# Two attention blocks over eight images: layer 1's first convolution in halves twice, its factors on GpSimd during attention, small norm products on GpSimd

## The chip, the cores and the metric

The kernel runs on one core of a Trainium2 chip. A core has five engines that work side by side, each with a queue that it takes in order: TensorE (PE: matmuls, with the weight loads shown as PEld), VectorE (DVE), ScalarE (ACT), GpSimd (POOL) and SyncE (SP), which here issues nearly all DMAs. They wait for each other by semaphores. The metric is the device time of one execution in microseconds. Before the change it is 2917.71 us, the median of three runs (2915.55 to 2919.3).

## The reference

The input is x with 8 images of 512 channels and 32 x 32 = 1024 positions, all in float32. Two layers follow each other:

```
layer 0:  h = group_norm(x, 32 groups);  q, k, v = w_qkv h + b   (8 heads of 64 channels)
          a = softmax(q^T k / 8) v for each head
          x = x + w_proj a + b_proj
layer 1:  h = group_norm(x, 8 groups)
          a = softmax(q^T k / sqrt(512)) v   (one head of 512 channels; q, k, v from 1x1 convolutions of h)
          out = x + w_p a + b
```

A 1x1 convolution is a product of a 512 x 512 weight with a 512 x 1024 image. In layer 1 the kernel multiplies weights once at the start: `m` joins those of q and k, so that the scores are h^T (m^T h), and `z` joins those of v and p. Layer 1 thus needs a first convolution g = m h (with the bias `ubias`), the scores of g and h, and a product with z.

## The kernel before, in words

**Products in seven instead of eight.** A product whose factors are cut in halves both ways takes eight products of the halves. `wino` (L227) makes it of seven, by Strassen's scheme in Winograd's form, from sums of halves: `left_sums` (L151) and `right_sums` (L165) give the steps: four kinds, each for two channel tiles, so eight additions or subtractions of 128x512 for an image. `image_factors` (L340) does that for an image with VectorE's `tensor_sub`. `conv` (L394) is a convolution that is halved once: seven products of four matmuls of 512 columns. A float32 matmul shows as two records in the profile, so that one product is eight records.

**Halved twice.** `conv2` (L416) halves each of the seven products again: 49 products of 128 x 128 weights with 256 columns. It takes them in four pairs: products 1 and 5, then 2 and 6, then 7 alone, then 3 and 4. Each pair goes through seven inner products; their results are added into the output tiles by VectorE (L439, from PSUM and from SBUF), with copies by ScalarE, and in the pair of product 7 by GpSimd as well (`more`, L443). It needs `inner_factors` (L400): for each of the seven outer factors four subtractions of 128x256, all on GpSimd (L411), and weights that `keep2` (L296) prepares once and stores in DRAM, read back in two parts. Before the change only layer 0's k and q convolutions are done so (of images 1 to 7); v, p, m and z are halved once. The bias is put on afterwards by ScalarE (`biased_half`, L446), one half of two output tiles at a time.

**Order of the work.** The loop over images b (L923) runs one stage after another: layer 0's attention of image b (`attention0`, L573), layer 1's first convolution of image b-1 (`layer1_scores`, L887), layer 0's projection of image b, the scores, z and the last product of image b-1, and v, k and q of image b+1. In the last round the previous image's layer 1 comes as always, and then that of the last image alone.

TensorE's matmuls are pinned to the order of the code (`matmul`, L66). The other engines' instructions are ordered by a planner of the language, which takes the earliest in the code that is ready by its own estimate, unless `tc.keep_in_program_order` pins one behind what stands before it on its engine. `background` is a list of small steps, of which a few are emitted after each product; `hooks` are steps emitted at given products; the last two products of a `wino` or of a pair wait in `tail` until the next one has begun.

**Attention of layer 0.** There are eight blocks (four pairs of heads, two halves of the queries). A block emits 16 score matmuls in eight steps, each followed by one exponential of 128x1024 on ScalarE (L590), whose results VectorE adds to a running total (L592, L594); then 16 matmuls with v; then `reciprocals` (L544): a matmul `sums` of the total with ones, VectorE's reciprocal `rc`, its minimum and (on GpSimd, L557) its sum kept for a check at the end, a DMA of `rc` to DRAM and back spread over partitions as `r`, and GpSimd's multiplication of the output by `r` (L611). The last block's multiplication is left to VectorE (`scaled`, L613). `extra` is a list of sixteen slots, two for each block: one emitted after the scores, one after the products with v. Before the change the slots 3, 5, 7 and 9 hold ScalarE's normalization (L140) of the next image to be treated, `h`; in image 0's attention the slots 0 to 6 hold the sums of the weights p, m and z, their stores (`keep`) and the first weight loads (`later`, L793).

**Memory.** All image tiles come from one pool of 32 buffers of 128x1024 (`big`, NBIG = 32, L19); weights from a pool of three (`wpool`). `uses` (L310) lists in which order the weights are loaded; each `load_weight` loads the next. PSUM pools are opened anew for each stage by `psum_pools` (L198).

**The norm.** `GroupNorm.affine` (L123) adds EPS on VectorE, takes the power -1/2 on GpSimd (L128), and then makes scale `s` and shift `b` by three VectorE instructions of 128x4 (L130, L132, L134).

Of the kernel before, what the change touches and what calls it, by code (L numbers as in the profile page):

```python
# [12 lines left out]
ALU = mybir.AluOpType  # L13
# [16 lines left out]
def two_attention_blocks_kernel(  # L30
# [41 lines left out]
    def pcols(name):  # L72
        i = 4 * PARAMS.index(name)
        return par[:, i : i + 4]
# [14 lines left out]
    class GroupNorm:  # L89
# [33 lines left out]
        def affine(self, ps):  # L123
            matmul(ps, gm[:, self.layer, :], self.dv, start=True, stop=True)
            ve = small.tile([P, KC], F32, tag="ve", name=f"ve_{self.uid}")
            nc.vector.tensor_scalar(ve, ps, EPS, None, ALU.add)  # L126
            rstd = small.tile([P, KC], F32, tag="rstd", name=f"rstd_{self.uid}")
            nc.gpsimd.tensor_tensor(rstd, ve, mhalf, ALU.pow)  # L128
            self.s = small.tile([P, KC], F32, tag="s", bufs=4, name=f"s_{self.uid}")
            nc.vector.tensor_mul(self.s, rstd, pcols(f"gn_w{self.layer}"))  # L130
            ms = small.tile([P, KC], F32, tag="ms", name=f"ms_{self.uid}")
            nc.vector.tensor_mul(ms, self.gmean, self.s)  # L132
            self.b = small.tile([P, KC], F32, tag="b", bufs=4, name=f"b_{self.uid}")
            nc.vector.tensor_sub(self.b, pcols(f"gn_b{self.layer}"), ms)  # L134

# [40 lines left out]
    def main_path(ctx):  # L176
# [113 lines left out]
        def keep(n, t):  # L290
            nc.sync.dma_start(wdram[n], t)


        wdram2 = {n: dram.tile([P, 7, 7, P], F32, name=f"sums2_{n}") for n in "qk"}

# [13 lines left out]

        twice = [("k", 0), ("k", 1), ("q", 0), ("q", 1)]  # L310
        uses = ["v", "p", *twice] if B > 1 else ["p"]
        for b in range(1, B):
            uses += ["m", "p", "z"] + (["v", *twice] if b + 1 < B else [])
        uses += ["m", "z"]
        loaded = []

        def load_weight():
            if uses:
                n = uses.pop(0)
                t = wpool.tile([P, 7 * C], F32, tag="w", name=f"w_{n[0]}_{len(uses)}")  # L320
                if n in twice:
                    t = t.rearrange("p (i j m) -> p i j m", i=4, j=7)
                    i = n[1]
                    t = t[:, : 4 - i]
                    nc.sync.dma_start(t, wdram2[n[0]][:, 4 * i : 4 + 3 * i])
                else:
                    t = t.rearrange("p (i k m) -> p i k m", i=7, k=2)
                    nc.sync.dma_start(t, wdram[n])
                loaded.append((n, t))
# [9 lines left out]

        def image_factors(h, uid):  # L340

            tiles = [pair_tile(f"t{i}_{uid}") for i in (1, 2, 4)]
            halves = lambda t: (t[:, :HT], t[:, HT:])
            return right_sums(
                [halves(t) for t in h[:2]], [halves(t) for t in h[2:]],
                [lambda j, t=t: t[:, j, :] for t in tiles], nc.vector.tensor_sub,
            )
# [67 lines left out]

        def conv2(n, f, bias, name, hooks=()):  # L416

# [28 lines left out]
            def biased_half(i, c):  # L446
                if bias is not None:
                    for r in range(2):
                        oc = 2 * i + r
                        t = out[oc][:, ts(c, HT)]  # L450
                        nc.scalar.activation(t, t, AF.Identity, bias=bias[:, oc : oc + 1])

# [86 lines left out]
            pair(2, (7,), [(1, 0)], [(0, 1)], [lambda: biased_half(1, 1)])  # L539
            pair(3, (3, 4), [(0, 1), (1, 0)], [(0, 1), (1, 0)], [load_weight, lambda: biased_half(0, 1), lambda: biased_half(1, 0)])  # L540
            return out
# [206 lines left out]
        def prologue():  # L748
# [44 lines left out]
            later = []  # L793
            for n in "pmz":
                t, steps = prepare(n)
                later.append(steps)
                later.append([lambda n=n, t=t: keep(n, t), load_weight])
            later.append([
                lambda: tc.keep_in_program_order(nc.vector.tensor_copy(ubias, bias[0])),
                lambda: tc.keep_in_program_order(nc.vector.tensor_add(obias[1], bias[1], pcols("bp1"))),  # L800
                lambda: tc.keep_in_program_order(nc.vector.tensor_add(obias[0], bias[2], pcols("bp0"))),
            ])
            return v, q, k, norm1, later

# [72 lines left out]
        def keys_and_queries(b, f, norm, hooks):  # L877

            k = conv2("k", f, None, f"k0_{b}", hooks)
            hooks = [[all_background], [], []]  # L880
            if norm:
                hooks[1].append(lambda: norm.group_mean(acc_tile(f"gmean_0_{b + 1}")[:, :KC]))
                hooks[2].append(lambda: norm.affine(acc_tile(f"gvar_0_{b + 1}")[:, :KC]))
            q = conv2("q", f, pcols("bq0"), f"q0_{b}", hooks)
            return q, k

        def layer1_scores(b, h, hooks):  # L887
            hf, steps = image_factors(h, f"h1_{b}")
            background.extend(steps)
            g = conv(  # L890
                weight("m"), hf, ubias, f"g1_{b}", middle=(2, 5, 6, 7), hooks=hooks, back=4,
                after=[load_weight, lambda: background.extend(gsteps)],
            )
            stiles = [pair_tile(f"sg{i}_{b}") for i in (1, 2, 4)]
            halves = lambda t: (t[:, :HT], t[:, HT:])
            gf, gsteps = left_sums(
                [halves(t) for t in g[:2]], [halves(t) for t in g[2:]],
                [lambda j, t=t: t[:, j, :] for t in stiles], nc.vector.tensor_add, nc.vector.tensor_sub,
            )
            return hf, gf  # L900

# [21 lines left out]
        for b in range(B):  # L923
# [11 lines left out]
            for i, f in enumerate(applies):  # L935
                extra[2 * i + 3].append(f)
            psum_pools(f"attention_{b}", 1)
# [4 lines left out]
            if b > 0:  # L942
                hf, gf = layer1_scores(b - 1, h, ends)
                norm1 = projection(b, af, xt)
# [6 lines left out]
                if b + 1 < B:  # L951
                    v, f, norm0 = values(b + 1, h)
                    q, k = keys_and_queries(b + 1, f, norm0, ())
            elif B > 1:
                v, f, norm0 = values(1, h, ends)
                norm1 = projection(0, af, xt)
                q, k = keys_and_queries(1, f, norm0, norm_hooks(norm1, "1_0")[1:])
            else:
                for f in sum(ends, []):
                    f()  # L960
                all_background()
                norm1 = projection(0, af, xt)
                finish()
                for f in sum(norm_hooks(norm1, "1_0"), []):
                    f()
                h, loads, applies = begun(load_again, norm1, 0, "h1")
                for f in loads + applies:
                    f()
        hf, gf = layer1_scores(B - 1, h, ())
        layer1_rest(B - 1, hf, gf, (), ())  # L970
# [196 lines left out]
```

## Time and profile before

The profiled execution took 2914.43 us, with a span of 2912.7 us and a granted TensorE clock of 1.00. The stages of one image, from the timeline and the sums over stretches (image 1's layer 1 beside image 2's layer 0; busy us of each engine):

| stage | from, to (us) | length | PE | DVE | ACT | POOL |
|---|---|---|---|---|---|---|
| attention of layer 0, 8 blocks | 688.00, 805.46 | 117.46 | 117.31 | 92.02 | 70.00 | 20.85 |
| first convolution of layer 1, most of the projection | 805.46, 847.30 | 41.84 | 41.65 | 30.04 | 3.85 | 0.98 |
| scores of layer 1 | 847.30, 895.80 | 48.50 | 48.50 | 28.33 | 8.43 | 2.58 |
| z and most of layer 1's last product | 895.80, 961.96 | 66.16 | 66.16 | 40.12 | 12.14 | 13.99 |
| v | 961.96, 1000.77 | 38.81 | 38.81 | 24.13 | 2.92 | 9.26 |
| k and q | 1000.77, 1045.20 | 44.43 | 43.16 | 26.19 | 11.39 | 12.26 |

A line of the timeline gives the start, the time from the first start to the last end, the engine, the line of the code, the operation, what it writes and reads, and how many instructions were merged; in brackets stands how long the engine was idle before and what ended that. In the lines of groups the mean duration of one comes after the busy time.

GpSimd's instructions that bear on the change, means over the run: 128x256 subtractions of the inner factors 734 to 1058 ns by kind (medians 722 to 727), 128x256 additions of `conv2` 724 to 727 ns, the 128x512 multiplication by `r` 2002 ns (1268 at least, 2352 at most), the power of 128x4 1018 ns, and the 128x896 sums of `keep2` about 2080 ns.

### The profile page before, as it was taken

How to read it: one execution, taken by the hardware profiler on the slowest of the kernel's cores; microseconds unless marked ns; L12 is line 12 of the kernel's file. 1: busy time of each engine (PE TensorE's matmuls, PEld its weight loads, DVE VectorE, ACT ScalarE, POOL GpSimd, SP SyncE). 2: the span in 40 equal slices, each digit the busy share in tenths (PEclk: the TensorE clock that was granted, in tenths of full speed). 3: DMA queues.
4: the chain of work that ended last, by engine and by line, in shares of the span. 5: the costliest groups of instructions: out<-in, count | busy, mean ns of one | idle time of the engine just before them, and what ended most of it. 6: DMA issues, size and time to landing. Idle time of an engine off the chain costs nothing.

```text
span 2912.7 us, 28999 instructions
## 1 busy us (share of the span) xinstructions
PE 2891.4 (99%) x10838; PEld 1495.4 (51%) x10838; DVE 1940.7 (67%) x2661; ACT 872.3 (30%) x1117; POOL 463.0 (16%) x477
## 2 busy tenths in 40 slices
PE   9999999999999999999999999999999999999999
PEld 5436534565345653457434574346733458334544
DVE  5488677566766568665776567866577665776555
ACT  1252451214512055121551115411164112631110
POOL 3023220032100312003210122102111031110000
PEclk9999999999999999999999999999999999999999
DMA  8433303223122231222212232122411223012201
GB/s 276 163 125 119 147 19 116 76 92 131 38 93 91 95 113 48 83 92 108 103 48 80 92 135 77 48 80 95 151 60 44 80 102 141 35 51 73 91 4 66
DMA packets 84186, 267.97 MB, mean 92 GB/s; under 512 B 10371, under 2 KB 29891, under 8 KB 75974
## 3 DMA queue, kind: packets, MB, share of 16 engines
q1 hardware_dynamic: 83622, 265.89, 25.2%
q8 instruction: 87, 1.43, 0.2%
q14 instruction: 61, 0.50, 0.1%
q10 hardware_dynamic: 416, 0.16, 0.0%
HBM read 216.30 MB, written 49.72 MB: 91 GB/s over the span
## 4 chain that ended last, share of the span: by engine, by line
PE 94%; DVE 2%; issue 1%; ACT 1%; POOL 1%; DMA 0%; SPq 0%; DVEq 0%; POOLq 0%; ACTq 0%
PE av L67 15%; PE sc L67 15%; PE psb_sc L67 6%; PE psb_av L67 6%; PE psa_av L67 4%; PE psa_sc L67 4%; PE psc_av L67 4%; PE psc_sc L67 4%; PE psb_z L67 3%; PE psb_p L67 3%; PE psb_g L67 3%; PE psb_v L67 3%; PE psb_k L67 3%; PE psc_z L67 2%; PE psa_z L67 2%; PE psc_p L67 2%
## 5 line engine op out<-in xcount | busy, mean ns | idle before, releaser
L594 DVE TENSOR_TENSOR sum<-sum,e 128x1024 f32<-128x1024 f32 x384 | 518.9, 1351 | 40.4 <-ACT e L590 0.5
L590 ACT ACTIVATE e<-sc 128x1024 f32<-128x1024 f32 x512 | 475.7, 1048 | 63.1 <-PE sc L67 63.1
L67 PE MATMUL sc<-q,k 64*128 64x512 f32 x2048 | 461.8, 598 | 1.1 <-ACT e L590 1.1
L67 PE MATMUL av<-e,v 128*64 128x512 f32 x2048 | 453.6, 595 | 0.0
L67 PEld LDWEIGHTS sc<-q,k 64*128 64x128 f32 x2048 | 188.1, 185 | 248.0 <-ACT e L590 124.0
L67 PEld LDWEIGHTS av<-e,v 128*64 128x64 f32 x2048 | 141.4, 137 | 304.3 <-issue 304.3
L557 POOL TENSOR_TENSOR all_recs<-all_recs,rc 128x256 f32<-128x256 f32 x72 | 64.6, 897 | 896.9 <-DVE rc L555 896.9
L555 DVE RECIPROCAL rc<-sums 128x256 f32<-128x256 f32 x72 | 126.4, 1756 | 88.0 <-PE sums L67 85.7
L611 POOL TENSOR_TENSOR a<-a,r 128x512 f32<-128x512 f32 x56 | 112.1, 2002 | 267.8 <-DMA r<-rows 258.3
L608 ACT COPY a<-av 128x512 f32<-128x512 f32 x64 | 37.5, 586 | 320.9 <-PE av L67 320.9
L642 ACT ACTIVATE e<-e 128x512 f32<-128x512 f32 x96 | 60.5, 630 | 232.6 <-DVE e L641 232.6
L592 DVE TENSOR_TENSOR sum<-e,e 128x1024 f32<-128x1024 f32 x64 | 78.4, 1226 | 66.3 <-ACT e L590 66.3
L67 PE MATMUL psa_sc<-g,h 128*128 128x512 f32 x256 | 115.7, 594 | 0.0
L67 PE MATMUL psa_av<-e,z 128*128 128x512 f32 x256 | 113.3, 595 | 0.0
L140 ACT ACTIVATE h<-h,b,s 128x1024 f32<-128x1024 f32 x62 | 78.6, 1270 | 58.1 <-DMA h<-in_x 46.6
L128 POOL TENSOR_TENSOR rstd<-ve,mhalf 128x4 f32<-128x4 f32 x16 | 16.3, 1018 | 499.9 <-DVE ve L126 499.9
L67 PE MATMUL psb_q<-inner_h,w_q 128*128 128x256 f32 x294 | 75.5, 385 | 6.5 <-DVE u_q L439 6.5
L67 PEld LDWEIGHTS psa_sc<-g,h 128*128 128x128 f32 x256 | 48.1, 190 | 57.9 <-issue 56.2
L67 PEld LDWEIGHTS psa_av<-e,z 128*128 128x128 f32 x256 | 48.0, 190 | 57.3 <-issue 55.4
L67 PE MATMUL psb_k<-inner_h,w_k 128*128 128x256 f32 x294 | 75.3, 383 | 0.0
L249 ACT COPY t_sc<-psa_sc 128x512 f32<-128x512 f32 x32 | 18.7, 586 | 181.7 <-DVE x L843 152.4
L444 POOL TENSOR_TENSOR k<-k,k 128x256 f32<-128x256 f32 x28 | 20.1, 727 | 291.1 <-DVE u_k L439 291.1
(304 smaller groups left out, 4582.9 us busy)
## 6 DMA issues: line engine op xcount, KB each, us to landing
x<-in_x SPq DMA_DIRECT2D x36, 512.0 KB
h<-in_x SPq DMA_DIRECT2D x32, 512.0 KB
r<-rows SPq DMA_DIRECT2D x128, 128.0 KB
spill<-x SPq DMA_DIRECT2D x32, 512.0 KB
h<-spill SPq DMA_DIRECT2D x32, 512.0 KB
x<-spill SPq DMA_DIRECT2D x32, 512.0 KB
out<-x SPq DMA_DIRECT2D x64, 256.0 KB
w_p<-sums_p SPq DMA_DIRECT2D x8, 1792.0 KB
```

The source lines that it names most:

```text
L67: tc.keep_in_program_order(nc.tensor.matmul(*args, **kw))
L140: tc.keep_in_program_order(nc.scalar.activation(dst, src, AF.Identity, bias=b, scale=s))
L249: nc.scalar.copy(t1[i], ps["a", i])
L444: nc.gpsimd.tensor_tensor(d, x, y, ALU.add)
L555: nc.vector.reciprocal(rc, sums)
L557: nc.gpsimd.tensor_tensor(all_recs, all_recs, rc, ALU.add)
L590: nc.scalar.activation(e, sc, AF.Exp, scale=(C // 8) ** -0.5)
L592: nc.vector.tensor_add(total, es[0], e)
L594: nc.vector.tensor_add(total, total, e)
L608: nc.scalar.copy(dst, av)
L611: nc.gpsimd.tensor_tensor(dst, dst, r, ALU.mult)
L642: nc.scalar.activation(dst, dst, AF.Exp, scale=scale)
```

## The change

It has three parts.

1. Layer 1's first convolution is done by `conv2` for images 0 to 6, and by `conv` as before for the last one. For that `keep2` prepares the weight m too, in the first attention; m's two parts stand in the list of uses, and the order of the preparations becomes p, z, m, with the weight loads placed anew. `conv2` gets `after`, steps to be emitted at its end.
2. The factors that this convolution needs are made during attention, by GpSimd: `image_factors` of `h` takes GpSimd's subtraction instead of VectorE's there (eight of 128x512), and the inner factors are made by GpSimd (28 of 128x256). The slots 9 to 13 of `extra` hold the eight and the first sixteen of the 28 (slot 9: two and four; 10: eight; 11: two and four; 12 and 13: two each); the other twelve go to the background at slot 15. ScalarE's normalizations move from the slots 3, 5, 7, 9 to 1, 3, 5, 7.
3. The norm's three small instructions go from VectorE to GpSimd. The query convolution's last two biases are emitted in the next attention's slot 0 instead of at the convolution's end (`late`), and all biases of `biased_half` are pinned in their order on ScalarE.

```diff
-            nc.vector.tensor_mul(self.s, rstd, pcols(f"gn_w{self.layer}"))
+            nc.gpsimd.tensor_tensor(self.s, rstd, pcols(f"gn_w{self.layer}"), ALU.mult)
...
-            nc.vector.tensor_mul(ms, self.gmean, self.s)
+            nc.gpsimd.tensor_tensor(ms, self.gmean, self.s, ALU.mult)
...
-            nc.vector.tensor_sub(self.b, pcols(f"gn_b{self.layer}"), ms)
+            nc.gpsimd.tensor_tensor(self.b, pcols(f"gn_b{self.layer}"), ms, ALU.subtract)
...
-        wdram2 = {n: dram.tile([P, 7, 7, P], F32, name=f"sums2_{n}") for n in "qk"}
+        wdram2 = {n: dram.tile([P, 7, 7, P], F32, name=f"sums2_{n}") for n in "qkm"}
...
-            uses += ["m", "p", "z"] + (["v", *twice] if b + 1 < B else [])
+            uses += [*twice["m"], "p", "z"] + (["v", *twice["k"], *twice["q"]] if b + 1 < B else [])
...
-        def image_factors(h, uid):
+        def image_factors(h, uid, sub=nc.vector.tensor_sub):
...
-        def conv2(n, f, bias, name, hooks=()):
+        def conv2(n, f, bias, name, hooks=(), after=(), late=None):
...
-                        nc.scalar.activation(t, t, AF.Identity, bias=bias[:, oc : oc + 1])
+                        tc.keep_in_program_order(nc.scalar.activation(t, t, AF.Identity, bias=bias[:, oc : oc + 1]))
...
-            pair(3, (3, 4), [(0, 1), (1, 0)], [(0, 1), (1, 0)], [load_weight, lambda: biased_half(0, 1), lambda: biased_half(1, 0)])
+            last = [lambda: biased_half(0, 1), lambda: biased_half(1, 0)]
+            if late is not None:
+                late += last
+                last = []
+            pair(3, (3, 4), [(0, 1), (1, 0)], [(0, 1), (1, 0)], [load_weight, *last, *after])
...
-            for n in "pmz":
+            for n in "pzm":
                 t, steps = prepare(n)
                 later.append(steps)
-                later.append([lambda n=n, t=t: keep(n, t), load_weight])
+                later.append([lambda n=n, t=t: keep(n, t)])
+            later[1].append(load_weight)
+            later[5].append(lambda: keep2("m", t))
...
+            later.append([load_weight, load_weight])
...
-            g = conv(
-                weight("m"), hf, ubias, f"g1_{b}", middle=(2, 5, 6, 7), hooks=hooks, back=4,
-                after=[load_weight, lambda: background.extend(gsteps)],
-            )
+            after = [lambda: background.extend(gsteps)]
+            if inner:
+                g = conv2("m", inner, ubias, f"g1_{b}", hooks, after)
+            else:
+                g = conv(weight("m"), hf, ubias, f"g1_{b}", middle=(2, 5, 6, 7), back=4, after=[load_weight, *after])
...
-                extra[2 * i + 3].append(f)
+                extra[2 * i + 1].append(f)
+            if b > 0:
+
+                hf, sums = image_factors(h, f"h1_{b - 1}", lambda *a: nc.gpsimd.tensor_tensor(*a, ALU.subtract))
+                inner, sums2 = inner_factors(hf, f"h1_{b - 1}")
+                extra[0] += late
+                for i, fs in enumerate((sums[:2] + sums2[:1], sums2[1:3], sums[2:4] + sums2[3:4], sums[4:6], sums[6:])):
+                    extra[9 + i] += fs
+                extra[15].append(lambda: background.extend(sums2[4:]))
```

## The prediction

> **What bounds the kernel now.** I read the page's busy shares first, then the waits of the TensorE queue, then the timeline of one image from 688 to 1045 us.
>
> ```profile
> PE 2891.4 (99%) x10838; PEld 1495.4 (51%) x10838; DVE 1940.7 (67%) x2661; ACT 872.3 (30%) x1117; POOL 463.0 (16%) x477
> ```
>
> TensorE's waits (total us, times, longest):
>
> ```profile
> PE psb_q L67 <- DVE u_q L439: 6.5, 6, 1.1
> ...
> PE psc_q L67 <- DVE c_q L439: 1.2, 6, 0.2
> PE sc L67 <- ACT e L590: 1.1, 7, 0.2
> ...
> PE psb_g L67 <- DVE u_g L238: 0.2, 1, 0.2
> ```
>
> TensorE is full: only fewer or shorter matmuls, or these small waits, can make the kernel faster, and any new wait in TensorE's own order is lost one for one. So I ask of each part whether it puts TensorE behind another engine.
>
> The matmuls that the change touches, in the timeline (start, us):
>
> ```profile
> 812.43 3.60 PE L67 MATMUL psc_g<-t_h,w_m 128*128 128x512 f32 x8
> 815.86 3.60 PE L67 MATMUL psb_g<-t_h,w_m 128*128 128x512 f32 x8
> ...
> 1002.50 1.03 PE L67 MATMUL psc_k<-inner_h,w_k 128*128 128x256 f32 x4
> 1003.36 1.03 PE L67 MATMUL psb_k<-inner_h,w_k 128*128 128x256 f32 x4
> ```
>
> Starts are to be compared, not durations: eight records of 512 columns take 3.43 us (0.429 each), four of 256 take 0.86 (0.216 each). The narrow form costs no extra.
>
> One attention block (of eight per image, 14.65 us each), and one contrast from the first block of another image, which has no multiplication on GpSimd:
>
> ```profile
> 761.50 7.14 PE L67 MATMUL sc<-q,k 64*128 64x512 f32 x32
> 764.70 1.23 DVE L592 TENSOR_TENSOR sum<-e,e 128x1024 f32<-128x1024 f32 x1 [0.80 <-ACT e L590]
> 766.03 8.75 DVE L594 TENSOR_TENSOR sum<-sum,e 128x1024 f32<-128x1024 f32 x6
> 768.76 2.28 POOL L611 TENSOR_TENSOR a<-a,r 128x512 f32<-128x512 f32 x1 [4.27 <-DMA r<-rows]
> 770.02 2.11 DVE L594 TENSOR_TENSOR sum<-sum,e 128x1024 f32<-128x1024 f32 x1
> 775.58 0.64 PE L67 MATMUL sums<-sum,ones 128*32 128x256 f32 x8
> ...
> 783.30 1.28 POOL L611 TENSOR_TENSOR a<-a,r 128x512 f32<-128x512 f32 x1 [4.15 <-DMA r<-rows]
> ...
> 1050.63 3.88 DVE L594 TENSOR_TENSOR sum<-sum,e 128x1024 f32<-128x1024 f32 x3
> ```
>
> VectorE's seven additions are a chain from the second exponential (764.70) to 774.78; the matmul `sums` needs the total and starts at 775.58. So VectorE has **0.80 us** to spare in a block, though its busy share is 67%. Three additions undisturbed take 3.88, a pitch of 1.33; six would take 7.87 and took 8.75. The 0.88 more is one addition that lasted 2.11 instead of 1.23 while GpSimd multiplied, and GpSimd's 128x512 took 2.28 instead of 1.28. **Each waits for the other.**
>
> **The skill.** The Trainium skill, "SBUF — State Buffer", section "Who interferes with whom", says that a VectorE instruction with two SBUF inputs contends with a GpSimd instruction that reads SBUF, and that one with at most one SBUF input does not; its section "SBUF: two separate sides" calls the shared pair an exclusive lock held for a whole instruction. The trace agrees: 0.88 us above, and in the k convolution, where VectorE reads one operand from PSUM, GpSimd's 128x256 additions keep their mean of 725 ns. A third case gives the price of a 128x256 subtraction on GpSimd to a VectorE instruction with two SBUF inputs:
>
> ```profile
> 959.45 0.69 DVE L681 TENSOR_TENSOR o<-psc_av,w_av 128x512 f32<-128x512 f32 x1
> 960.17 1.22 DVE L682 TENSOR_TENSOR o<-o,r 128x512 f32<-128x512 f32 x1
> 960.81 1.17 POOL L411 TENSOR_TENSOR inner_h<-h 128x256 f32<-128x256 f32 x1
> ```
>
> 1.22 against 0.69 is **0.53 us**.
>
> **Part 1, layer 1's first convolution (7 of 8 images).** Before: 7 products of 8 records, 56 x 0.429 = 24.03 us. After: 49 of 2 records, 98 x 0.216 = 21.16. Gain 2.87 an image, **-20.1 us** in all. The last image keeps the old form.
>
> VectorE's share of it grows. A twice halved convolution has 30 VectorE instructions and 13.6 us of VectorE time (420 instructions of L439 over 14 convolutions), most in its second half; the old one had ten of 0.69 to 0.75. Into that second half fall the last scaling (0.69) and the attention output's eight subtractions (8 x 0.6): from the third pair's first product to the fourth's, VectorE has about 8.5 us of work for 4.7 us of matmuls, with two PSUM buffers a bank between. Bounds: 0 if the buffers take it all, 3 us if little; the q convolution lost 1.1 + 0.2 us for a VectorE delay of 2.57. I take 1.0 an image, **+7**.
>
> The sums' last biases now stand on ScalarE ahead of `g`'s sums (4 x 0.72 = 2.9 us); before, `sg` was begun at 832.84 and read by TensorE at 861.04, so that hides. Weights: `m` comes as 1792 and 1344 KB instead of 1792; three buffers still run three uses ahead, and `p`, `z` are called a stage early; DMA is 14% busy in attention. Free.
>
> **Part 2, factors on GpSimd inside attention (7 images).** Removed from VectorE: 8 x 0.69 at the end of attention, where TensorE waited 0.2 us in the whole run; nothing to win. Added to GpSimd in blocks 4 to 6 (from 0): 8 subtractions 128x512 (1.27 clean) and 16 of 128x256 (0.72), 21.7 us; 12 more of 128x256 after the last block, beside PSUM readers, first used two pairs later: free.
>
> GpSimd has room, but VectorE's additions hold the lock. GpSimd is free of them only from 774.78 to the next block's 779.35: 4.57 less 0.90 for `all_recs`, 3.7 us, five 256s. GpSimd works in order, and after the multiplication ends (771.04) two gaps are left before the last two additions. By block:
> - 4: two 512s in the two gaps, 2 x 0.88 - 0.80 = 0.96 us on TensorE; four 256s in the free window.
> - 5: two 256s, 1.06 - 0.80 = 0.26; five in the window.
> - 6: one 256 is left, and slot 11 has two 512s and four 256s, ahead of `all_recs` in the queue: 5 x 0.53 + 2 x 0.88 = 4.41. The block's own multiplication, in the 0.80 already, slips to the window: 4.41 - 0.88 - 0.80 = 2.73.
> - 7: of slots 12 and 13's four 512s one fits the window: 3 x 0.88 - 0.80 = 1.84.
>
> Sum 5.8. The planner may float these to when `h` is ready (in the values stage `inner_h` ran at 948, over 10 us ahead of the first `v` matmul at 961.96 that its place in the code follows). The same tally from readiness gives 0.6 in block 1, 1.7 in 2, 0.3 in 3, 3.4 in 4: 6.0. Lower bound: all in windows, 0; upper: all 24 in gaps, 8 x 0.88 + 16 x 0.53 less 4 x 0.80 = 12.3. I take 5.8: **+41 us**.
>
> The applications of `h` move one block earlier on ScalarE, which is busy 8 of 14.65 us; image 1's first load is issued at 116.28, the first application would come at 127 and ScalarE's next work at 133. Free.
>
> **Part 3, norm and biases.**
>
> ```profile
> 1038.43 1.02 POOL L128 TENSOR_TENSOR rstd<-ve,mhalf 128x4 f32<-128x4 f32 x1
> 1039.48 0.68 DVE L130 TENSOR_TENSOR s<-rstd,par 128x4 f32<-128x4 f32 x1 [2.57 <-POOL rstd L128]
> 1041.94 1.13 PE L67 MATMUL psb_q<-inner_h,w_q 128*128 128x256 f32 x4 [1.08 <-DVE u_q L439]
> ```
>
> VectorE waits 2.57 us for GpSimd's power, with five additions of q queued behind it, and TensorE then 1.08 for `u_q`. With the three small ones on GpSimd, VectorE doesn't stop. They cost GpSimd 0.17 (1.27 and 0.72 drawn down to no columns) to 1.02 us each, ahead of q's own additions there; so of 7.7 us I count **-6** (-7.7 to 0). The late biases free ScalarE 2.56 us ahead of the first exponential: **-1.1**, the whole wait of `sc`; they have till 1060.7, the second block. Once, `m`'s inner sums on GpSimd (4 x 2.08 of 128x896, as for q and k) beside the first attention's additions: **+2** (0 to 6), and seven stores of 448 KB on SP, behind which `rows` and `r` may wait; their reader is GpSimd's multiplication, not TensorE.
>
> **Sum**: -20.1 + 7 + 41 - 6 - 1.1 + 2 = +23. The durations are of the profiled run (span 2912.7, time 2914.4), 3.3 under the median of the other three; on 2917.7 this makes **2941 us**.
>
> **Rivals.**
> - Additions held up (forecast, 0.62): 2941, own range 2926 to 2965.
> - The lock is mostly missed (0.30): GpSimd's work falls into free windows and block stalls stay under 2 us an image. For it: 3.7 us a block over seven blocks are 26 us against 21.7. Against: work comes in strings of six to eight and starts where additions still run. -20.1 - 7.1 + 2 with 0 to 7 for part 1 and up to 9 of block stalls: 2893 to 2909, say 2900. It ends faster; the sign turns at (20.1 + 6 + 1.1 - 7 - 2) / 7 = 2.6 us of block stalls an image, 3.6 if part 1 stalls nothing.
> - A near balance (0.04): stalls of 1.8 to 3.4 an image, 2912 to 2923.
> - The buffers run out (0.04): attention holds 16 long tiles and 9 for exponentials of 32 in block 4, and the change adds up to ten. If exponentials wait for a buffer in two blocks an image, some 2 x 2 us x 7 = +28 more: 2969.
>
> Faster and slower are told apart here by 0.2% (6 us). Faster 0.32, within 0.04, slower 0.64. The range takes in the faster case: 2893 to 2962.
>
> **What would show it.** Right: `sums` in TensorE's waits, on VectorE's addition, some 40 us in all; L594's mean well above its 1351 ns (41 us lost and 4 x 0.80 x 7 = 22 us of spare time used up, over 384 additions: some 1500); GpSimd's 128x512 subtractions near 2 us; `psb_q`'s wait nearly gone; `g`'s records at a pitch of 0.216. Wrong: L594's mean unchanged and no wait of `sums`, or a wait of `g`'s matmuls above 10 us.

## The result and the profile after

The changed kernel takes 2950.95 us (median of four runs, 2950.16 to 2952.07), the kernel before 2918.51 beside it: a ratio of 1.0113, 95% interval 1.0096 to 1.0131. It is slower, by 32 us between the medians and by 36.4 us between the two profiled spans (2949.1 against 2912.7). The ledger below is made on the spans. The forecast of 2941 had the sign and the main mechanism. It is 10 us low: two losses were put too low, against one loss put too high and a gain put too low.

The busy shares of the changed kernel:

```profile
PE 2878.9 (98%) x11132; PEld 1554.4 (53%) x11132; DVE 2014.1 (68%) x2697; ACT 923.9 (31%) x1201; POOL 866.6 (29%) x837
```

TensorE's busy time fell by 12.5 us and the span rose by 36.4, so it now waits. GpSimd is busy 404 us longer and VectorE 73 us longer (the time in which one stands behind the other counts as busy), though the change takes instructions away from VectorE's attention. What TensorE waits for (total us, times, longest):

```profile
PE sums L67 <- DVE sum L598: 37.8, 29, 4.4
PE psb_g L67 <- ACT psb_g L477: 5.6, 7, 0.8
PE psb_g L67 <- DVE u_g L439: 5.3, 7, 1.0
...
PE psb_g L67 <- DVE g L439: 3.7, 7, 0.5
PE psc_g L67 <- DVE c_g L439: 3.5, 7, 0.5
...
PE psc_q L67 <- DVE c_q L439: 0.4, 1, 0.4
```

New are `sums`, and four waits in each of the seven doubly halved convolutions with m, 18.1 us together. Gone are the waits of psb_q (6.5) and of sc (1.1). The additions of the exponentials, in the groups:

```profile
L598 DVE TENSOR_TENSOR sum<-sum,e 128x1024 f32<-128x1024 f32 x384 | 569.7, 1484 | 41.3 <-ACT q L451 0.5
```

1484 ns in the mean, against 1351 before. Two attention blocks, in which GpSimd works on the factors (start, time from first start to last end):

```profile
762.23 10.52 DVE L598 TENSOR_TENSOR sum<-sum,e 128x1024 f32<-128x1024 f32 x6 [0.46 <-DVE sum L596]
...
765.06 2.18 POOL L615 TENSOR_TENSOR a<-a,r 128x512 f32<-128x512 f32 x1 [4.66 <-DMA r<-rows]
...
767.21 4.46 POOL L946 TENSOR_TENSOR t_h<-h 128x512 f32<-128x512 f32 x2
...
771.63 1.71 POOL L411 TENSOR_TENSOR inner_h<-h 128x256 f32<-128x256 f32 x1
...
772.80 0.64 PE L67 MATMUL sums<-sum,ones 128*32 128x256 f32 x8 [1.25 <-DVE sum L598]
...
777.98 11.00 DVE L598 TENSOR_TENSOR sum<-sum,e 128x1024 f32<-128x1024 f32 x6
...
782.86 3.38 POOL L411 TENSOR_TENSOR inner_h<-t_h 128x256 f32<-128x256 f32 x2
...
786.20 1.70 POOL L411 TENSOR_TENSOR inner_h<-t_h,inner_h 128x256 f32<-128x256 f32 x1
...
789.04 0.64 PE L67 MATMUL sums<-sum,ones 128*32 128x256 f32 x8 [1.51 <-DVE sum L598]
```

The six additions that took 8.75 us before take 10.52 and 11.00. GpSimd's 128x512 takes 2.23 (1.27 alone) and its 128x256 1.70 (0.72 alone): each finishes only when an addition has had its turn. In the seven later blocks of this image `sums` starts at 727.52, 742.17, 756.83, 772.80, 789.04, 805.41 and 820.48: 14.65 us a block until block 3, then 15.97, 16.24, 16.37 and 15.07.

The spans cut by stages show where the 36.4 us lie. An attention runs from the start of its first score matmul to the start of its last matmul with v; "between" is the time from there to the next attention, so the last block's wait of `sums` falls into it. The last row ends with the start of the last matmul.

| stretch | before | after | sum of the differences |
|---|---|---|---|
| up to image 0's attention | 118.8 | 119.9 | +1.1 |
| image 0's attention | 116.1 | 123.6 | +7.5 |
| seven attentions, each | 117.0 | 120.6 to 121.0 | +25.6 |
| first between | 95.1 | 93.6 | -1.5 |
| six later betweens, each | 238.3 to 240.8 | 240.1 to 240.8 | +1.7 |
| after the last attention | 316.0 | 317.9 | +1.9 |

The betweens hold losses and gains that nearly cancel, which only experiments can separate. The first row is within the scatter: with the same code up to there, the profiles of the kernel before and of its version with late biases differ by 1.6 us (118.8 and 120.4).

### The profile page after: what moved, and what is told of

The parts are those of the page before. It is cut to its first block, busy times and chain, and to the rows that moved or that the text cites. A ratio compares the mean times of both kernels' runs of the same rounds, so it can differ in the third digit from the quotient of the medians.

```text
span 2949.1 us, 30211 instructions
## 1 busy us (share of the span) xinstructions
PE 2878.9 (98%) x11132; PEld 1554.4 (53%) x11132; DVE 2014.1 (68%) x2697; ACT 923.9 (31%) x1201; POOL 866.6 (29%) x837
## 4 chain that ended last, share of the span: by engine, by line
PE 82%; DVE 14%; issue 2%; ACT 2%; POOL 0%; DVEq 0%; ACTq 0%; POOLq 0%
DVE sum L598 10%; PE sc L67 9%; PE av L67 8%; PE psb_sc L67 6%; PE psb_av L67 6%; PE psa_av L67 4%; PE psa_sc L67 4%; PE psc_av L67 4%; PE psc_sc L67 4%; PE psb_z L67 3%; PE psb_p L67 3%; PE psb_v L67 3%; PE psb_k L67 3%; PE psb_q L67 2%; PE psb_g L67 2%
## 5 line engine op out<-in xcount | busy, mean ns | idle before, releaser
L598 DVE TENSOR_TENSOR sum<-sum,e 128x1024 f32<-128x1024 f32 x384 | 569.7, 1484 | 41.3 <-ACT q L451 0.5
L67 PEld LDWEIGHTS sc<-q,k 64*128 64x128 f32 x2048 | 194.0, 187 | 240.6 <-ACT e L594 105.2
L561 POOL TENSOR_TENSOR all_recs<-all_recs,rc 128x256 f32<-128x256 f32 x72 | 76.6, 1064 | 658.6 <-DVE rc L559 658.6
L596 DVE TENSOR_TENSOR sum<-e,e 128x1024 f32<-128x1024 f32 x64 | 90.6, 1415 | 48.5 <-ACT e L594 48.5
L411 POOL TENSOR_TENSOR inner_h<-h 128x256 f32<-128x256 f32 x56 | 75.5, 1348 | 151.3 <-PE psc_av L67 151.3
L411 POOL TENSOR_TENSOR inner_h<-h,inner_h 128x256 f32<-128x256 f32 x112 | 95.0, 852 | 0.5
L67 PE MATMUL psb_g<-inner_h,w_m 128*128 128x256 f32 x294 | 76.3, 388 | 14.6 <-ACT psb_g L477 5.6
L411 POOL TENSOR_TENSOR inner_h<-t_h 128x256 f32<-128x256 f32 x84 | 87.5, 1057 | 0.0
L411 POOL TENSOR_TENSOR inner_h<-t_h,inner_h 128x256 f32<-128x256 f32 x84 | 83.5, 993 | 2.1
```

Source lines behind the costliest of these rows:

```text
L67: tc.keep_in_program_order(nc.tensor.matmul(*args, **kw))
L411: nc.gpsimd.tensor_tensor(dst, x, y, ALU.subtract)
L561: nc.gpsimd.tensor_tensor(all_recs, all_recs, rc, ALU.add)
L596: nc.vector.tensor_add(total, es[0], e)
L598: nc.vector.tensor_add(total, total, e)
```

## The experiments

Unless said otherwise times are medians, and ratios are to the kernel before, run on the same chip (median 2915.16 for the first four kernels, 2915.15 for the next three, then 2914.67 and 2919.13). The prediction's theory: GpSimd's reading of SBUF holds up VectorE's additions. Its rivals among causes: the place of the work in GpSimd's queue (behind it wait `all_recs` and the multiplication by `r`), or the ten more buffers.

### No factors at all

```diff
-                hf, sums = image_factors(h, f"h1_{b - 1}", lambda *a: nc.gpsimd.tensor_tensor(*a, ALU.subtract))
-                inner, sums2 = inner_factors(hf, f"h1_{b - 1}")
...
+                hf = {1: b11, 2: b21, 3: b22, 4: b22, 5: b12, 6: b22, 7: b12}
...
+                for p, (fst, snd) in hf.items():
+                    (c11, c12), (c21, c22) = quarters(fst, 2 * P), quarters(snd, 2 * P)
+                    inner[p] = {1: c11, 2: c21, 3: c22, 4: c22, 5: c12, 6: c22, 7: c12}
...
-                    extra[9 + i] += fs
```

> The kernel after, with the 36 subtractions on GpSimd left out in each of seven images: layer 1's first convolution reads unsubtracted quarters of h, so what it computes is not the reference's; the matmuls, their shapes and their order stay, and 10 buffers an image are not taken. Theory (GpSimd's subtractions hold the SBUF port that VectorE's additions of exponentials need): of the 37.8 us that TensorE waits for the sum only the 4.4 us in image 0 stay, and the time falls by some 33 us to about 2917. Rival (the twice halved convolution itself, or the moved biases and normalizations, cost the time): 2940 or more. Rival (the pool of 32 buffers is short): falls as well; this run can't tell it from the theory, the next one does.

Measured: 2916.38, ratio 0.9999 (0.9991 to 1.0008). The 36 subtractions an image cost **34.6 us** (2950.95 - 2916.38). By the stages from image 1's attention on it is 36.3: this kernel's profile holds 3.3 us in its first between that the changed kernel's lacks, a loss of another kind that is treated under "VectorE shut out for 6 us". All waits of `sums` but one in image 0 are gone; m's convolution still waits 16.6 us, so those waits have another cause.

### About the same time on GpSimd, writing only

Each subtraction is replaced by fills of 128x256 (0.31 us each) into the same buffer: two for a 128x256, four for a 128x512. That is about the time that the subtractions take alone.

```diff
+        def fill(dst, n):
+            for i in range(n):
+                nc.gpsimd.memset(dst[:, : 2 * P] if i % 2 or dst.shape[-1] == 2 * P else dst[:, 2 * P :], 0.0)
...
-                        nc.gpsimd.tensor_tensor(dst, x, y, ALU.subtract)
+                        if fill is None:
+                            nc.gpsimd.tensor_tensor(dst, x, y, ALU.subtract)
+                        else:
+                            fill(dst, 2)
...
+                hf, sums = image_factors(h, f"h1_{b - 1}", lambda d, x, y: fill(d, 4))
+                inner, sums2 = inner_factors(hf, f"h1_{b - 1}", fill)
```

> The kernel after, with each of the subtractions replaced by two or four fills of 128x256 with zeros on GpSimd, into the same buffers, at the same places and for about the same time (0.31 us a fill: 0.62 for a 128x256, 1.24 for a 128x512); the values are not the reference's. GpSimd reads nothing in them. Theory (the shared read port): VectorE's additions go on at 1225 ns, the waits for the sum shrink to image 0's 4.4 us plus little, about 2917. Rival (GpSimd's queue is too full, its multiplications and their successors come late, or buffers are short): the fills take the same time and buffers, so 2945 to 2951.

Measured: 2918.70, ratio 1.0004 (0.9995 to 1.0012). The wait of `sums` in TensorE's waits of this kernel:

```profile
PE sums L67 <- DVE sum L605: 4.4, 1, 4.4
```

The additions in the groups of the kernel without factors (busy us and mean ns of one after the count):

```profile
L598 DVE TENSOR_TENSOR sum<-sum,e 128x1024 f32<-128x1024 f32 x384 | 522.8, 1361 | 41.4 <-ACT e L594 0.9
```

The same group in the kernel that only writes:

```profile
L605 DVE TENSOR_TENSOR sum<-sum,e 128x1024 f32<-128x1024 f32 x384 | 524.0, 1364 | 41.1 <-ACT q L458 0.5
```

The same places in the queue, the same buffers, and fills beside the additions for 2.0 to 3.6 us in each of four blocks, and the additions keep 1364 ns. So it is what GpSimd reads: neither the queue nor the buffers. The Trainium skill, "SBUF — State Buffer", section "Who interferes with whom", says that a VectorE instruction with two SBUF inputs contends with a GpSimd instruction that reads SBUF and not with one that only writes it; both halves are seen here.

### The factors in the free windows

The first sixteen inner subtractions and the eight of 128x512 are pinned on GpSimd behind the block's last addition, by a copy of one column of the total; four more inner ones too, and the four sums of `keep2("m")` are taken two at a time in two windows.

```diff
+                        seen = small.tile([P, 1], F32, tag="seen", name=f"seen_{uid}")
+                        pool(nc.gpsimd.tensor_copy(seen, total[:, 1, HT - 1 : HT]))
+                        for f in fs:
+                            f()
```

> The kernel after with the same 36 subtractions, but 24 of them (28 with four of the background's) pinned on GpSimd in groups, one group at the end of each of the first seven blocks, behind a copy of one column of the running total, which waits for the block's last addition: they run in the 4.6 us in which VectorE adds nothing. The sums for m's inner weights in image 0 likewise, two at a time. Theory: the waits for the sum go nearly all, in image 0 too: 2951 - 33 - 4.4 - 3.4 (the slower TensorE clock behind image 0's wait, if the wait causes it) = about 2910. Rival (the amount of GpSimd work counts, not its place): above 2940.

Measured: 2913.28, ratio 0.9994 (0.9987 to 1.0001), 37.7 us under the changed kernel with the same arithmetic; 5.1 of them lie in image 0's attention. The attentions of images 1 to 7 take 116.5 to 116.9 us and image 0's 118.5. So the prediction's second rival, that the lock is mostly missed, was a matter of where the work stood: the same subtractions cost 35 us in the planner's places and some 2 us in the windows (116.5 to 116.9 in seven attentions, against 116.4 in the kernel without factors). What is left is m's convolution, with its 18.1 us of waits unchanged.

### Part 3 alone, and each half of it

Three kernels are the kernel before with part 3's edits: all of it, the three norm instructions alone, the late biases alone. Their diffs are those lines of the change.

> The kernel before with part 3 alone: the norm's three small instructions on GpSimd, the last two biases of q in the next attention, biases pinned. Theory: TensorE's waits for u_q and c_q (7.7 us) and for the first exponentials (1.1 us, and some refill) go: 2918.5 - 9 = 2909 to 2912. Rival (the small instructions delay GpSimd's own additions for q, and the prologue's norm gets longer): 2917 to 2920.

> The kernel before with the three norm instructions on GpSimd, and nothing else. Part 3 alone gave -10.3 us, where the prediction had -6 for the norm and -1.1 for the late biases. From the trace of the changed kernel the q stage is 1.12 us an image shorter. Theory that this is the norm's: psb_q's wait of 6.5 gone, 7 x 1.1 = 8 us less, 2907. Rival that the prediction's -6 holds and the biases carry the rest: 2909. A once-only loss of 5 us from VectorE's t_a beside GpSimd's string (as in e3_part3) may come in or not, and is seen in the trace.

> The kernel before with the late biases (and their order pinned on ScalarE) alone. The prediction said -1.1 us in all: the whole wait of sc. In part 3's trace the attention of images 1 to 7 is 116.4 us against 117.0. Theory that this 0.6 an image is theirs: 7 x 0.6 = 4, 2911, attention 116.4. Rival that only the shown wait of 1.1 us goes: 2914, attention 116.8 or more. psb_q's waits of 6.5 us should stay in both.

| kernel | time | ratio (95%) | q stage of images 1 to 6 | attention, 1 to 7 |
|---|---|---|---|---|
| before | | | 25.62 to 25.73 | 117.0 |
| part 3 | 2904.87 | 0.9957 (0.9941, 0.9974) | 24.13 to 24.24, once 24.59 | 116.4 |
| norm | 2909.29 | 0.9977 (0.9968, 0.9985) | 24.14 to 24.24, once 24.59 | 117.0 to 117.3 |
| late biases | 2910.36 | 0.9984 (0.9975, 0.9994) | 25.62 to 25.73 | 116.4 |

(The q stage is counted from its first weight load to the attention's first matmul.) The norm is worth 1.49 us (25.73 to 24.24) in a q stage, 8.9 us in six, where the waits shown were 7.7; why the loss is longer than the waits is not shown. The norm alone gives 0.2 us an attention back, since sc then waits 2.3 us instead of 1.1 for the first exponential; with the late biases that wait is gone. In its own time the norm alone gains 5.4 us (2914.67 to 2909.29), which is the rival's figure and not the theory's 2907; its profile's first between is 3.2 us longer than before, by the loss that the kernel without factors has there too. So the 8.9 us stand on the stages alone. The late biases give 0.65 us an attention, 4.5 us in all, as expected of the theory and four times the wait that the profile put on sc. In image 2's attention the first exponential starts 0.94 us earlier, and that block alone is 0.64 shorter. The edit also pins the order of the biases, which was not tried apart. Part 3 alone came out under the 2909 to 2912 that were expected; they were counted from 2918.5, and the gain of 10.3 us is near the 9 that were reckoned with. It is a better kernel than before, and by 46 us better than the whole change.

### The waits in m's convolution

Two edits on the kernel with windows: the order of the first pair when nothing is left to finish, and then also the attention output's scaling and eight subtractions emitted later.

```diff
+                order = (6, 2, 5, 7) if tail else (5, 6, 2, 7)
                 finish()
-                for j in (6, 2, 5, 7):
+                for j in order:
```
```diff
-                gf = layer1_scores(b - 1, hf, inner, ends)
+                (scaled, extend) = ends[1]
+                gf = layer1_scores(b - 1, hf, inner, [[], [scaled], [], [extend, lambda: run_background(4)]])
```

> v1_windows with the one edit of the order of inner products in the first pair (5, 6, 2, 7 when nothing is left to finish, 6, 2, 5, 7 otherwise); the scaling and the eight subtractions stay where they are. If ScalarE's copy is a separate cause, its 5.6 us (0.8 an image) go and the waits on VectorE (12.5 us) stay: 2913 - 6 = 2907. If the copy's wait is only the first of a chain that VectorE sets anyway, the time is lost again at the next wait: 2911 to 2914, with VectorE's waits grown to 16 or more.

> The kernel with pinned factors (v1_windows) still waits 18.1 us in m's convolution, 2.6 an image: 5.6 for ScalarE's copy of psb_g into PSUM, which stands at the start with no product of another pair to cover it, and 12.5 for VectorE's additions, behind which the attention output's last scaling and eight subtractions are queued. Here both are moved: the first pair takes product 5 before 6, 2 and 7 when nothing is left in the tail, and the scaling and the eight subtractions are emitted two pairs later (the scaling in the second pair, the subtractions after the convolution's last). Theory that these two causes make the waits: psb_g, psc_g waits under 4 us in all, time 2913 - 18 to - 25, so 2888 to 2897, faster than the kernel before and than its version with part 3 alone (2905). Rival that the convolution's own 13.6 us of VectorE time in 21 us are the cause: the waits stay above 12 us, 2905 to 2913. Rival that the work comes back as a wait in the projection, for the subtractions: psb_p waits over 10 us, 2905 or more.

The order alone: 2908.03, ratio 0.9976 (0.9964 to 0.9987), 5.3 us less; the wait for ScalarE's copy is gone and those for VectorE stay. Both: 2896.34, ratio 0.9929 (0.9912 to 0.9945), 17 us less than with windows alone. What is left in the convolution, of 18.1 us:

```profile
PE psb_g L67 <- DVE u_g L461: 1.5, 7, 0.2
```

The stage from m's first matmul to the first score matmul, as most images have it:

| kernel | m and most of the projection | against before's 41.30 |
|---|---|---|
| changed kernel, and with windows | 42.17 | +0.87 |
| and the order | 41.38 | +0.08 |
| and the later subtractions | 39.29 | -2.01 |

The matmuls alone are 2.87 shorter. So the convolution lost 3.75 us an image to waits, of which 0.8 stood behind ScalarE's copy, 2.1 behind the output's scaling and subtractions on VectorE, and 0.9 is left. This theory of the waits stands; that the convolution's own VectorE time makes them is refuted for all but that 0.9, whose cause is open, and no wait came back in the projection from image 1 on. Part of the backlog is the same exchange with GpSimd as in the attention: beside the 128x256 additions of product 7's pair the last four of the eight subtractions take 0.87 to 1.21 us instead of 0.68, some 1.1 us together. In the later places some 0.9 us of that stays, while TensorE's shown waits are 0.2 us an image, so the place counts more than this exchange.

### A TensorE clock that falls after a wait

In the changed kernel's first attention, where `keep2("m")` runs on GpSimd:

```profile
165.25 10.37 POOL L306 TENSOR_TENSOR prepare_m<-prepare_m 128x896 f32<-128x896 f32 x4 [5.02 <-DVE prepare_m L286]
...
182.42 1.08 PE L67 MATMUL sums<-sum,ones 128*32 128x256 f32 x8 [4.41 <-DVE sum L598]
183.43 9.69 PE L67 MATMUL sc<-q,k 64*128 64x512 f32 x32
```

The wait is 4.41 us, and after it the 32 score records take 9.69 instead of 7.14 and the eight of `sums` 1.08 instead of 0.64. To see whether the wait is the cause, the kernel before got waits of growing length, one an image.

```diff
+                    if (hp, tb) == (2, 0):
+                        for _ in range(b):
+                            nc.vector.tensor_tensor(total, total, total, ALU.max)
```

> The kernel before, with VectorE made late by a known time in one attention block an image: in the fifth block of image b, b in-place maxima of the total with itself (128x1024, 1.23 us each, values unchanged) before the sums. TensorE should wait 1.23 b - 0.8 us there: about 0.4, 1.7, 2.9, 4.1, 5.4, 6.6, 7.8 us in images 1 to 7. Theory that a wait above some 2 to 3 us makes TensorE's clock 0.5 for some microseconds after it: the stretches after the waits of images 1 and 2 show clock 1.00, those after images 3 or 4 to 7 show about 0.5 for 3 to 7 us, and the attention of those images grows by the wait plus 2 to 4 us. Rival that the drop in image 0's attention belongs to something else there (the work of the prologue, GpSimd's sums, DMA traffic): clock 1.00 after every wait, and each attention grows by its wait alone.

The matmuls of `sums` in the timeline, after the waits of images 1 to 5:

```profile
404.23 0.64 PE L67 MATMUL sums<-sum,ones 128*32 128x256 f32 x8 [0.40 <-DVE sum L611]
...
763.62 0.64 PE L67 MATMUL sums<-sum,ones 128*32 128x256 f32 x8 [2.02 <-DVE sum L611]
...
1124.56 1.08 PE L67 MATMUL sums<-sum,ones 128*32 128x256 f32 x8 [2.91 <-DVE sum L611]
...
1487.55 1.08 PE L67 MATMUL sums<-sum,ones 128*32 128x256 f32 x8 [4.19 <-DVE sum L611]
...
1852.90 1.08 PE L67 MATMUL sums<-sum,ones 128*32 128x256 f32 x8 [5.43 <-DVE sum L611]
```

Sums over stretches of 7 us from the end of the waits of images 2, 3 and 4 (the stretch, its length, the busy us of PE, PEld, DVE, ACT and POOL with their counts, then the granted clock, the DMA share and GB/s):

```profile
763.00:770.00 7.00, 6.38 (x36) 2.77 (x36) 5.20 (x5) 4.57 (x6) 0.90 (x1) 1.00 0.07 20
1124.00:1131.00 7.00, 6.44 (x30) 2.69 (x32) 3.91 (x4) 3.25 (x4) 0.90 (x1) 0.76 0.04 13
1487.00:1494.00 7.00, 6.45 (x24) 2.64 (x26) 3.23 (x4) 2.47 (x3) 0.90 (x1) 0.58 0.01 2
```

| image | 1 | 2 | 3 | 4 | 5 | 6 | 7 |
|---|---|---|---|---|---|---|---|
| wait of `sums`, us | 0.40 | 2.02 | 2.91 | 4.19 | 5.43 | 7.05 | 7.96 |
| attention, above 117.0 | 0.5 | 2.1 | 4.4 | 6.8 | 8.0 | 8.6 | 9.7 |
| more than the wait | 0.1 | 0.1 | 1.5 | 2.6 | 2.6 | 1.6 | 1.7 |

Up to 2.02 us a wait costs itself. From 2.91 us the clock is 0.5 for some microseconds (one record of 3.4 us after 2.91, 6.8 after the longer ones), and the wait costs 1.5 to 2.6 us more than itself. The rival, that the drop belongs to image 0, falls. There is one wait of each length, and the length alone does not settle it: in image 0 the changed kernel's 4.41 was followed by 6.8 us of half clock, the 4.43 of the kernel that only writes by 3.4. The Trainium skill, "TensorE: Matmul & The Clock Gate", section "What's actually happening", describes half the clock after an idle window of about 3.4 us, and a free-running window; here the measurement differs: 2.91 us was enough, and 2.70 in the next experiment, though not always.

### VectorE shut out for 6 us

The kernel with windows and both edits had one loss that the kernel with windows had not: 98.7 us in its first between, against 93.6. The timeline of VectorE and GpSimd there, and TensorE's next matmuls:

```profile
258.17 0.74 POOL L433 TENSOR_TENSOR inner_h<-h 128x256 f32<-128x256 f32 x1
258.20 6.04 DVE L170 TENSOR_TENSOR t_a<-a 128x512 f32<-128x512 f32 x1
258.85 1.42 POOL L433 TENSOR_TENSOR inner_h<-h,inner_h 128x256 f32<-128x256 f32 x2
260.22 0.73 POOL L433 TENSOR_TENSOR inner_h<-h,h 128x256 f32<-128x256 f32 x1
260.91 0.73 POOL L433 TENSOR_TENSOR inner_h<-h,inner_h 128x256 f32<-128x256 f32 x1
261.59 1.42 POOL L433 TENSOR_TENSOR inner_h<-t_h 128x256 f32<-128x256 f32 x2
262.95 1.87 POOL L433 TENSOR_TENSOR inner_h<-t_h,inner_h 128x256 f32<-128x256 f32 x2
...
269.88 5.73 PE L67 MATMUL psb_p<-t_a,w_p 128*128 128x512 f32 x8 [2.70 <-DVE v L397]
```

A subtraction that takes 0.67 us a little later lasts 6.04, while eight of GpSimd's follow each other at their undisturbed 0.69; it ends inside the ninth. TensorE waits 2.70 us, and its next eight records take 5.73 instead of 3.60. The profiles of four other kernels (no factors, writing only, part 3, norm) hold the same: a subtraction of 6.03 to 6.08 us and a wait of 2.69 to 2.74. After three of these waits the clock was 0.5 for 3.4 us as well. In the kernel without factors it stayed at 1.00, and the eight records took 4.04:

```profile
273.93 4.04 PE L67 MATMUL psb_p<-t_a,w_p 128*128 128x512 f32 x8 [2.69 <-DVE v L375]
```

The edit gives image 0's (and only image 0's) eight subtractions of the attention output to GpSimd, at the head of that string; it was put into this kernel and, alone, into the kernel before.

```diff
+            if b == 0:
+                af, steps = image_factors(a, f"a_{b}", lambda *x: nc.gpsimd.tensor_tensor(*x, ALU.subtract))
...
+                    background[:0] = steps
...
+                return af, [[], [scaled, ahead_of_all]]
```

> v2_windows_order lost some 5 us once, between the attentions of images 0 and 1 (98.7 us against 93.6 in v1_windows): a VectorE subtraction of 128x512 on the output of the attention (t_a) lasted 6.04 us instead of 0.6 to 0.7, beside a string of 128x256 subtractions of GpSimd that follow each other without a gap; TensorE then waited 2.70 us and its clock was 0.5 for 3.4 us. Here the eight subtractions of image 0's attention output go to GpSimd itself, ahead of the rest of its string, so that no VectorE instruction with two SBUF operands stands beside the string. Theory (VectorE is kept out by GpSimd's string): no VectorE instruction above 3.2 us in the run, no such wait, no half clock, 94 us between the attentions, 2896 - 5 = 2891. Rival (GpSimd becomes late with image 1's inner factors by the 8 x 1.27 us, or projection waits for GpSimd's t_a): a new wait of psa_k, psb_k or psb_p on GpSimd of several us, 2896 or more.

> The kernel before with one edit: the eight subtractions of image 0's attention output on GpSimd, ahead of its string of inner factors. The unprofiled runs of the kernel before lie in two groups, 2913.6 to 2916 and 2917 to 2921; its profiled run, in the lower group, has no long VectorE subtraction. Theory that the upper group are runs in which VectorE's subtraction is kept out for 6 us by GpSimd's string (as in the profiles of four other kernels): here all runs lie within some 3 us, at 2912 to 2915, beside runs of before in both groups. Rival that the two groups have another cause: both groups are here too, 4 to 5 us apart.

In the kernel with all edits: 2891.37, ratio 0.9915 (0.9898 to 0.9931), 5.0 us less than without this one; first between 93.6, no VectorE instruction above 3.1 us and no half clock before the kernel's end. **This is the best kernel of the study**, 23 us under the kernel before and 60 under the changed one.

In the kernel before the edit alone gives 2915.07, ratio 0.9991 (0.9982 to 0.9999), and something else: 13 runs from 2914.2 to 2916.5. The 17 runs of the kernel before beside them lie in two groups, seven from 2914.4 to 2915.6 and ten from 2919.1 to 2920.6, with nothing between. The upper group is gone with the string's competitor. So the 4.5 us by which the kernel before scatters come from these subtractions beside the string. That it is the one long instruction is argued: no profile shows that kernel in its upper group. Other kernels' profiles agree: that of the norm alone has the long subtraction and lies in the upper part of its runs (2913.57, where nine of 13 lie from 2907.3 to 2910.2), those of the kernel before and of the one with windows lack it and lie in the lower.

## Why the prediction was right, and where its sizes were wrong

The signs of all parts came as argued; the sum was +23 and the span grew by 36.4. By its steps:

| step | predicted | measured | from |
|---|---|---|---|
| m's matmuls | -20.1 | -20.1 | g's records keep the pitch of 0.216 us |
| waits in m's convolution | +7 | +26 | 3.75 x 7, the stage's length less the matmuls' gain |
| additions held up | +41 | +34.6 | the kernel without factors (36.3 by stages) |
| q's waits, by the norm | -6 | -8.9 | 1.49 x 6 |
| late biases | -1.1 | -4.5 | 0.65 x 7 |
| `keep2("m")` in image 0 | +2 | +7.5 | image 0's attention |
| sum | +23 | +35 | against +36.4 |

**Additions held up: right in kind and nearly in size.** `sums` waits 37.8 us, 33.4 without image 0 (some 40 said); the additions' mean is 1484 ns (1500 said), and GpSimd's 128x512 takes 2.23 us (near 2 said). The tally by blocks 4 to 7 was 0.96, 0.26, 2.73 and 1.84; the blocks were 1.32, 1.59, 1.72 and 0.42 longer than 14.65. The work ran earlier than its slots, so that block 5 carried what block 7 should have, and the price of a 128x256 was too high: an addition beside one took 1.57 us instead of 1.23, 0.34 more, where the prediction took 0.53 from a 128x512 of VectorE. A 128x512 cost its 0.88. The windows show that the second rival's premise (room enough in the gaps) was true and its conclusion not: without a pin, GpSimd started while the additions ran.

**Waits in m's convolution: the step that was mis-sized most.** The prediction took 1.0 an image and 3 at most; they are 3.75, and the sign by which it said it would be wrong there, over 10 us in g's waits, appeared (18.1). The backlog of VectorE behind the scaling and the eight subtractions was named, and is 2.1 of it. Not named was ScalarE's copy psb_g, 0.8: when this convolution opens a stage there is no product of another in the tail to run while the copy is made. And the loss was put at the length of the waits, while TensorE loses more: 2.6 us of shown waits went with 3.75 us of time, as 7.7 us of shown waits in q went with 8.9.

**Image 0.** The sums on GpSimd were thought to cost 0 to 6. They cost a wait of 4.41 and then, 7.5 less 4.4, about 3 us more, in 6.8 us at half clock. The profile before could not show that: its attentions hold no TensorE wait above 0.2 us.

**Part 3** was better than predicted in both halves, 13 us for 7 by the stages (10.3 in the time of part 3 alone). The rival of the buffers is not needed: filling the same buffers without reading costs nothing.

So two errors of opposite sign, +24.5 from waits and image 0 against -12.7 from the lock and part 3, left 13 us on the spans (with 1.6 that no row holds, about what the stages put on the lock above its 34.6). That the sum came so near is in part luck. Three of the 13 the forecast had gained by standing on the median of 2917.7, above the profiled run.

## What to carry to other kernels

Before work is moved to GpSimd beside VectorE instructions with two SBUF operands, find the windows in which those don't run and pin the work into them: the same subtractions cost 35 us in the planner's places and some 2 us in the windows. A matmul form that saves TensorE time has to be charged with what its results need from VectorE and ScalarE at that place in the order, above all at the start of a stage, where nothing covers the first copy; and a TensorE wait of about 2.7 us or more has to be charged with half a clock that may follow it. A kernel whose runs fall into two groups may hold one race between two engines, to be looked for as a single long instruction in a profile of the upper group.

## What had not been expected of the hardware

- TensorE's clock was 0.5 for 3.4 to 6.8 us after four of five single waits of 2.69 to 2.74 us and after each of 2.91 and more (the kernel's start aside), and not after 2.02. From 2.91 on this cost 1.5 to 2.6 us on top of the wait. What decides near 2.7 stays open.
- The lock between GpSimd and VectorE does not alternate where GpSimd's instructions follow each other closely: VectorE was kept out for 6 us, over eight of them, in five profiles. In the attention it did alternate, one addition to each GpSimd instruction. The Trainium skill, "SBUF — State Buffer", section "SBUF: two separate sides", says that the first to start has the pair for its whole instruction; that the next one of the same engine can follow it is what these runs add. Why the two stretches differ stays open.
- The norm's three instructions of 128x4 take GpSimd 0.20 us each, at the lower end of the 0.17 to 1.02 that the prediction allowed, although the power of the same shape beside them takes 1.02 (medians).
